# Six row products for four rows in the offset convolution, and its preparation one band earlier

## The chip, the cores and the metric

One core of a Trainium2 chip runs the whole kernel. The metric is the device time of one execution in microseconds. The engines are TensorE (PE; its weight loads are shown as PEld), VectorE (DVE), ScalarE (ACT), GpSimd (POOL) and SyncE (SP); POOL and SP also issue DMAs. Each engine takes its instructions in the order of the program.

## What is computed

Input x is 8 images of 128 channels by 64 x 64, all float32. Layer 0 normalises x by groups, computes 27 offset and mask channels with a 3 x 3 convolution, samples the image at the shifted places (a modulated deformable convolution), and adds the batch-normalised result to x. Layer 1 does a mixture of convolutions and isn't touched.

```python
om = conv3x3(gn(x), off_w) + off_b          # 27 channels a pixel
off, mask = om[:, :18], sigmoid(om[:, 18:])
val = bilinear samples of gn(x) at (y + ky - 1 + off_y, x + kx - 1 + off_x), times mask
y = sum over taps and channels of w * val + b
x = x + relu(batchnorm(y))
x = x + layer1(gn(x))
```

## The kernel before

**Bands.** `dense` walks over 64 bands, 8 (NB) for each image, each of 8 rows. `g` is the number of a band, `b, j` its image and its place in the image. A band has two parts. First come five sample groups: `weights` (L698) multiplies column and row weights on VectorE three groups ahead, `sample` runs the products on TensorE (L714, tile pq, three buffers) and ScalarE copies them away (L724). Then come the nine taps of the convolution of the band before it (`conv`, L763, tile py, one buffer). In band 0 the band before is the last of the previous image; it has two stretches of rows, and so eighteen matmul taps, which count as nine parts of two.

**Between the taps** the loop puts other work, by the number of the part (0 to 8). `pixels` (parts 0, 1, 5, 6) transposes picked pixels into pt (L672), and ScalarE copies them out (L677); pt and the tiles of the offset convolution share one buffer in ps_c. `spread` works on column weights, on ScalarE (L648, parts 1 and 5) and on VectorE (L650, parts 3 and 7). `pick` (L657) stands at part 4. `load_quarter` loads a quarter of the image two ahead, at part 4 of bands 2 to 5, on SP's queue.

**Loads of tables.** In the sample groups of each band POOL issues two column loads (`load_x`, L632) and eight row loads (`load_y`, L617).

**Tables of the next image but one.** `tables(b)` is a generator; after each tap the loop asks it for its next steps, three times (four in the first image's bands, and in band 0 three for each part of two taps). It yields BLOCK where it needs the shared buffer, and goes on from there only at the parts in BLOCKS. Its steps are: the group mean (pm, L309, and d, e, gm on VectorE), the group variance (pv, L319, and ve, L322), the power on POOL (L325), shift on VectorE (L328), the affine on the eight chunks of the image, in place, by turns on ScalarE (L332) and VectorE (L336), and then the offset convolution. `statistics(b)` (bn_stats, L294, and mv, L297) comes ahead of it.

**Offset convolution.** It takes two output rows at a time. Four combinations of input rows are made on VectorE (`combine`, L360, two halves of 128 x 1024 each), and each goes through 3 column taps x 4 quarters of the image, each quarter in 32 output columns of the array, on 8 rows of 64 (L379). The results are put together in om as even and odd rows (L402 to L415). om is turned by ScalarE (L422) and stored by SP's queue (L427, L432); later steps load it again (L465, L452) and make the tables (L503 to L564).

Of the kernel before, what the change touches and what calls it, by code (L numbers as in the profile page):

```python
# [8 lines left out]
F32 = mybir.dt.float32  # L9
I32 = mybir.dt.int32  # L10
AF = mybir.ActivationFunctionType
ALU = mybir.AluOpType
# [4 lines left out]
P = 128  # L17
H = W = 64
# [4 lines left out]
CH = 512  # L23
# [6 lines left out]
NE = 4  # L30
# [16 lines left out]
NB = NROW // 2  # L47
# [4 lines left out]
ROWPAD = REACH  # L52
# [4 lines left out]
BLOCK = "block"  # L57
# [7 lines left out]
def deform_moe_conv(  # L65
# [18 lines left out]
    nc = tc.nc  # L84
    B = x.shape[0]
# [92 lines left out]
    def dense():  # L178

        with ExitStack() as st:  # L180
# [16 lines left out]
            nc.gpsimd.memset(offw_sb[:, :, 27:32], 0.0)  # L197

            offu_sb = [a1.tile([P, 3, 32], F32, name=f"offu_sb{i}") for i in range(2)]
            offb_sb = a1.tile([P, 1], F32, name="offb_sb")  # L200
            nc.gpsimd.memset(offb_sb, 0.0)
            ident = a1.tile([P, P], F32, name="ident")
# [60 lines left out]
            def pause(n):  # L263
                for _ in range(n):
                    yield
# [34 lines left out]
            def tables(b):  # L300
# [22 lines left out]
                yield from pause(3)  # L323
                scale = small.tile([P, 1], F32, name="scale")
                nc.gpsimd.tensor_tensor(scale, ve, nhalf, ALU.pow)  # L325
                yield from pause(8)
                shift = small.tile([P, 1], F32, name="shift")
                nc.vector.scalar_tensor_tensor(shift, gm, -1.0, scale, ALU.mult, ALU.mult)  # L328
                yield
# [69 lines left out]
                for j in (1, 2):  # L399
                    yield from combine(j)  # L400
                yield from block(1)
                nc.scalar.activation(even, taken(1), AF.Identity, bias=offb_sb)  # L402
                yield from combine(0)
                yield from block(2)
                if b == 0:
                    yield from combine(3)
                m2 = taken(2)
                nc.vector.tensor_tensor(odd, even, m2, ALU.subtract)
                nc.vector.tensor_tensor(even, even, m2, ALU.add)
                if b:  # L410
                    yield from combine(3)
                yield from block(0)
                nc.vector.tensor_tensor(even, even, taken(0), ALU.add)
                yield from block(3)
                nc.vector.tensor_tensor(odd, odd, taken(3), ALU.subtract)  # L415
                yield
# [412 lines left out]
            load_x(2, nc.gpsimd)  # L829
            made, means_of = later, iter(())  # L830
            asked = False
            PIXELS, BLOCKS, SPREAD = (0, 1, 5, 6), (2, 3, 4, 7), (1, 3, 5, 7)

            def put_off():

# [10 lines left out]
            for g in range(len(bands) + 1):  # L846
                b, j = bands[g] if g < len(bands) else (B, 0)
                if j == NB - 2:
                    for _ in made:
                        pass  # L850
                    asked, made, means_of = True, iter(()), statistics(b + 2)
                turned = pixels(g + 1) if g + 1 < len(bands) else iter(())
                for q in range(NGR):
                    if g < len(bands):
                        if g or q + AHEAD < NGR:
                            weights(g * NGR + q + AHEAD)
                        sample(g * NGR + q)
                        if q == 2:
                            load_x(g + 3, nc.gpsimd)
                        if q in (2, 3):  # L860
                            for k in range(T * (q - 2), T * (q - 1)):
                                load_y(g + 2, k, nc.gpsimd)
                    if q == 1:
                        put_off()
                taps = conv(g - 1) if g else iter(())
                twice = 2 if g and bands[g - 1][1] == NB - 1 else 1
                for done, _ in enumerate(taps):
                    part, odd = divmod(done, twice)
                    if odd == 0 and part in PIXELS:
# [12 lines left out]
                    for _ in range(3 + (g < NB) if twice == 1 else 1 + done % 2):  # L882
                        tick()
                    if odd == 0 and part == 4:
                        if g + 2 < len(bands):
                            pick(g + 2)
                        if 2 <= j < 6:
                            load_quarter(b + 2, j - 2)
                for _ in turned:
                    pass  # L890
                if g == 0:
                    pick(2)
                    for slots in HALVES:
# [238 lines left out]


    def layer1():
        yscale = small.tile([P, 1], F32, name="yscale")
        rsqrt(yscale, ymv[:, 1:2], BN_EPS)
        nc.vector.tensor_tensor(yscale, yscale, gamma_sb, ALU.mult)
        yshift = small.tile([P, 1], F32, name="yshift")
        nc.vector.tensor_tensor(yshift, ymv[:, 0:1], yscale, ALU.mult)
        nc.vector.tensor_tensor(yshift, beta_sb, yshift, ALU.subtract)  # L1140
        with ExitStack() as st:
# [59 lines left out]
            def prepare(b, made):  # L1201
# [98 lines left out]
                tot = small.tile([P, 1], F32, name="tot")  # L1300
                nc.vector.tensor_reduce(tot, wd, AX.X, ALU.add)
                nc.vector.reciprocal(tot, tot)
                nc.vector.tensor_scalar(wd, wd, tot, None, ALU.mult)
                bmix = small.tile([P, 1], F32, name="bmix")

                def mix_biases():
                    mb = small.tile([P, NE], F32, name="mb")
# [194 lines left out]
```

## Time and profile before

| | |
|---|---|
| three timed runs, us | 1516.3, 1513.72, 1515.72; median 1515.72 |
| the profiled execution, us | 1504.96 (its span 1503.2) |
| mean granted TensorE clock | 0.969 |
| L379, offset convolution, after image 0 | 672 passes of 504 or 512 columns, 586 to 617 ns each, overlapping |
| L360, combinations on VectorE | 61 of 128x1024, 1229 ns, 73.3 us |
| L336 / L332, affine of a chunk, VectorE / ScalarE | 545 / 808 ns |
| L294, bn_stats of a chunk | 64, 678 ns |
| L325, power on POOL | 8, 647 ns |
| L677, copy of four transposed pixel tiles | 585 ns |
| L724, copy of a sample group | 923 or 1051 ns |
| column loads, row loads on POOL's queue | 576 KB each, 7.6 us to landing; 90 KB each, 8.1 us |

The profile describes one execution on the chip, and its times are from the span's start. A line of a timeline names the start, the length, the engine, the line of the kernel, the operation, the tiles written and read, and how many instructions were merged (x24); brackets give idle time of the engine ahead of it and what ended it. A float32 matmul shows as two passes. Matmuls are pipelined, so the length of one overlaps with the next; the distance between starts tells more.

### The profile page before, as it was taken

How to read it: one execution, taken by the hardware profiler on the slowest of the kernel's cores; microseconds unless marked ns; L12 is line 12 of the kernel's file. 1: busy time of each engine (PE TensorE's matmuls, PEld its weight loads, DVE VectorE, ACT ScalarE, POOL GpSimd, SP SyncE). 2: the span in 40 equal slices, each digit the busy share in tenths (PEclk: the TensorE clock that was granted, in tenths of full speed). 3: DMA queues.
4: the chain of work that ended last, by engine and by line, in shares of the span. 5: the costliest groups of instructions: out<-in, count | busy, mean ns of one | idle time of the engine just before them, and what ended most of it. 6: DMA issues, size and time to landing. Idle time of an engine off the chain costs nothing.

```text
span 1503.2 us, 21231 instructions
## 1 busy us (share of the span) xinstructions
PE 1363.5 (91%) x7714; PEld 761.6 (51%) x7714; DVE 959.3 (64%) x1906; ACT 818.3 (54%) x1095; POOL 449.9 (30%) x745
## 2 busy tenths in 40 slices
PE   4279799999999999999999899999994999999998
PEld 1245465556555555555556555566551444444443
DVE  5555475576557657656764775554528887888882
ACT  2365674776577468658656865866634232322320
POOL 6333242443334244333423333343303010110100
PEclk9589899999999999999999999999996999999999
DMA  4486775986697498669748866788708345665411
GB/s 143 115 181 126 175 163 105 213 190 137 128 202 179 95 196 214 137 130 207 187 99 183 194 147 135 168 183 200 171 26 248 93 124 149 168 168 154 110 45 58
DMA packets 130939, 227.27 MB, mean 151 GB/s; under 512 B 82003, under 2 KB 88303, under 8 KB 122137
## 3 DMA queue, kind: packets, MB, share of 16 engines
q0 software_dynamic: 54960, 137.08, 43.9%
q1 hardware_dynamic: 74848, 88.25, 19.9%
q8 instruction: 63, 1.03, 0.3%
q10 hardware_dynamic: 1017, 0.50, 0.1%
q14 instruction: 51, 0.42, 0.1%
HBM read 180.23 MB, written 45.35 MB: 150 GB/s over the span
## 4 chain that ended last, share of the span: by engine, by line
PE 53%; DMA 12%; ACT 9%; issue 9%; DVE 7%; SPq 2%; POOL 1%; ACTq 0%; DVEq 0%; POOLq 0%
PE py L763 20%; PE pc L1414 12%; PE pq L714 11%; PE pc L379 5%; PE pt L672 4%; DMA xwts<-tabx 4%; DMA pad<-in_x_dram 2%; ACT xwts L648 2%; ACT xt L677 2%; DMA combo<-colwise 2%; ACT work L537 1%; DMA x<-in_x_dram 1%; DMA yd<-y 1%; ACT samples L724 1%; DMA combo<-rowwise 1%
## 5 line engine op out<-in xcount | busy, mean ns | idle before, releaser
L763 PE MATMUL py<-samples,dw_sb 128*128 128x512 f32 (+3 forms) x1296 | 577.3, 562 | 7.1 <-ACT y L771 5.3
L617 POOL DMA_DIRECT2D ywts<-taby x504 | 305.5, 624 | 279.6 <-DMA xwts<-tabx 228.3
L714 PE MATMUL pq<-s,xt 64*128 64x144 f32 (+1 forms) x3840 | 283.8, 301 | 35.8 <-DVE s L698 24.7
L714 PEld LDWEIGHTS pq<-s,xt 64*128 64x128 f32 x3840 | 257.6, 190 | 84.7 <-ACT samples L724 24.2
L724 ACT COPY samples<-pq 128x864 f32<-128x864 f32 (+1 forms) x320 | 280.7, 974 | 33.6 <-PE pq L714 33.3
L763 PEld LDWEIGHTS py<-samples,dw_sb 128*128 128x128 f32 x1296 | 217.1, 190 | 160.3 <-issue 133.3
L677 ACT COPY xt<-pt 128x512 f32<-128x512 f32 (+1 forms) x256 | 142.4, 556 | 209.7 <-PE pt L672 209.2
L698 DVE TENSOR_TENSOR s<-xwts,ywts 128x72 f32<-128x72 f32 (+1 forms) x447 | 199.4, 499 | 84.6 <-PE pq L714 43.6
L650 DVE TENSOR_SCALAR xwts<-xwts 128x1152 f32<-128x1152 f32 (+2 forms) x130 | 97.3, 749 | 186.6 <-ACT xwts L648 186.2
L672 PEld LDWEIGHTS pt<-ident,picked 128*128 128x128 f32 x960 | 110.9, 141 | 171.7 <-ACT xt L677 105.0
L1414 PE MATMUL pc<-v,u 128*128 128x512 f32 x384 | 175.8, 605 | 6.3 <-DVE v L1321 6.3
L672 PE MATMUL pt<-ident,picked 128*128 128x128 f32 x960 | 152.8, 279 | 29.6 <-ACT xt L677 27.1
L632 POOL DMA_DIRECT2D xwts<-tabx x128 | 72.8, 573 | 353.5 <-DVE s L698 276.8
L1414 PE MATMUL pc<-v,wmix 128*128 128x512 f32 x384 | 174.0, 598 | 0.0
L648 ACT ACTIVATE xwts<-xwts,place 128x1152 f32<-128x1152 f32 (+2 forms) x130 | 160.9, 1242 | 11.5 <-DMA xwts<-tabx 11.5
L1392 ACT ACTIVATE t<-pc,bmix 128x512 f32<-128x512 f32 x32 | 22.0, 687 | 189.2 <-PE pc L1414 100.5
L1414 PEld LDWEIGHTS pc<-v,u 128*128 128x128 f32 x384 | 72.7, 192 | 93.5 <-issue 84.7
L1414 PEld LDWEIGHTS pc<-v,wmix 128*128 128x128 f32 x384 | 72.3, 190 | 91.4 <-issue 89.6
L360 DVE TENSOR_TENSOR combo<-pad 128x1024 f32<-128x1024 f32 x61 | 73.3, 1229 | 23.0 <-PE pc L379 14.4
L657 DVE COPY picked<-pad 128x960 f32<-128x960 f32 x128 | 81.9, 681 | 0.0
L771 ACT ACTIVATE y<-py,db_sb 128x512 f32<-128x512 f32 (+3 forms) x72 | 45.7, 635 | 65.6 <-PE py L763 31.1
L837 DVE BATCH_NORM_STATS2 ystats<-y 128x6 f32<-128x512 f32 (+3 forms) x72 | 44.5, 626 | 21.0 <-ACT y L771 21.0
(173 smaller groups left out, 955.3 us busy)
## 6 DMA issues: line engine op xcount, KB each, us to landing
xwts<-tabx POOLq DMA_DIRECT2D x128, 576.0 KB, 7.6
ywts<-taby POOLq DMA_DIRECT2D x504, 90.0 KB, 8.1
pad<-in_x_dram SPq DMA_DIRECT2D x36, 512.0 KB
out_dram<-yo SPq DMA_DIRECT2D x32, 512.0 KB
yd<-y SPq DMA_DIRECT2D x48, 256.0 KB
pad<-yd SPq DMA_DIRECT2D x16, 512.0 KB
x<-yd SPq DMA_DIRECT2D x16, 512.0 KB
x<-in_x_dram POOLq DMA_DIRECT2D x16, 512.0 KB, 9.2
```

What stands on the lines that cost most here:

```text
L379: nc.tensor.matmul(pcs[j][32 * q : 32 * q + 32].rearrange("p (h w) -> p h w", w=W)[:, :, lo:hi], lhsT=weight_of[j][:, kx], rhs=combo_of[j] ...
L617: engine.dma_start(out=y_wts[g % 2][at : at + NR * Q, r].rearrange("p a b c -> p (a b c)"), in_=bass.AP(tensor=y_table[b].tensor, offset=y ...
L648: nc.scalar.activation(part, part, AF.Abs, bias=column)
L650: nc.vector.tensor_scalar(part, part, -1.0, 0.0, ALU.add, ALU.min)
L657: nc.vector.tensor_copy(picked[g % 2][:, :, h], bass.AP(tensor=one.tensor, offset=one.offset, ap=[list(one.ap[0]), [T, NCOL], [W, Q], [1, Q]],
L672: nc.tensor.transpose(pt[:, c], picked[g % 2][:, c0 + c].rearrange("p h y x -> p (h y x)"), ident,)
L677: nc.scalar.copy(xts[g][:, c0 : c0 + n], pt[:, 0:n])
L698: engine.tensor_tensor(s[:, :, 3 * at : 3 * (at + k)].rearrange("p m (c x) -> p m c x", x=3), by_x[:, :, c : c + k], by_y[:, :, w : w + k] ...
L714: nc.tensor.matmul(by_m[:, h, :, at : at + k], lhsT=xts[g][rows, c], rhs=s[rows, :, at : at + k], start=True, stop=True,)
L724: nc.scalar.copy(bass.AP(tensor=one.tensor, offset=one.offset + first, ap=[list(one.ap[0]), [M * PLANE, 2], [PLANE, M], [WB + 1, 3], [1, w ...
L763: nc.tensor.matmul(py, lhsT=dw_sb[:, 3 * (2 - yy) + 2 - xx], rhs=samples[g % 2][:, m : m + 3 * n - 2 : 3, xx, 1 : W + 1], start=(i == 0), ...
L1414: nc.tensor.matmul(pc, lhsT=us[j][:, kx], rhs=vs[g][:, rows, kx : kx + W], start=(kx == 0), stop=(kx == 2),)
```

## The change

From the third image on (b of 2 and up) the offset convolution takes four output rows at a time: six combinations of six input rows, six products with six combinations of the three weight rows, and sums of the products. The combinations come in pairs, four VectorE operations each on 128 x 1024 (`combine_pair`); a pair of products (`pair`) shares a tile, 256 columns for each, and has 2 x 3 x 4 matmuls on 4 rows of 64. The six weight combinations (`quad_of`, `quad_weights`) are made once, after band 5 of image 0, in place, with one new tile. Images 0 and 1 keep the four products.

The steps ahead of the convolution are moved, for images 2 to 7. Counting the yields gives these places, with three steps a part (image 2, with four steps in bands 6 and 7, has its shift at part 1):

| step | before | after |
|---|---|---|
| bn_stats of chunks 0 to 5 | band 6, parts 0 to 5 | the same |
| bn_stats of chunks 6, 7, and mv | band 7, parts 0, 1 | band 6, part 6 |
| pm; d, e, gm | band 7, part 2 | band 6, part 7 |
| pv; ve | band 7, part 3 | band 6, part 8 |
| power on POOL | band 7, part 4 | band 7, part 0 |
| shift | band 7, part 7 | band 7, part 2 |
| affine chunks | band 7, parts 7, 8; band 0, part 0 | band 7, parts 2, 3, 4 |
| combinations | band 0, parts 1 to 3, 7, 8; band 1, parts 2, 3 | the first in band 7, part 8; seven in band 0, parts 0 to 4; four in band 1, parts 0 to 2 |
| products | block 1: band 0, part 7; blocks 2, 0, 3: band 1, parts 2, 4, 7 | pair 0: band 0, part 7; pairs 1, 2: band 1, parts 3, 7 |
| results into om | after each block | two after pair 0 (and one on ScalarE), two after pair 1 (and one on ScalarE), six after pair 2 |
| turning, stores and all that follows | from band 1, part 8 | the same |

Four small tiles of the layer-1 part get one buffer where they had two (not shown in the diff).

```diff
+            offv_sb = a1.tile([P, 3, 32], F32, name="offv_sb")
+            quad_of = (
+                offw_sb[:, 0:3], offu_sb[0], offu_sb[1], offw_sb[:, 3:6], offv_sb, offw_sb[:, 6:9]
+            )
...
-                yield from pause(8)
+                yield from pause(8 if b < 2 else 6)
                 shift = small.tile([P, 1], F32, name="shift")
...
+                PACE = 2, 2, 2
+                quad = omr.rearrange("p (t i w) -> p i t w", i=4, w=W)
+                halves = [(t[:, 0 : H // 4], t[:, H // 4 :]) for t in combos]
+                def row(k):
+                    return pad[:, ROWPAD - 1 + k :][:, 0 : H - 3 : 4]
+                def mix(out, a, times, c):
+                    if times in (1, -1):
+                        op = ALU.add if times == 1 else ALU.subtract
+                        nc.vector.tensor_tensor(out, c, a, op)
+                    else:
+                        nc.vector.scalar_tensor_tensor(out, a, float(times), c, ALU.mult, ALU.add)
+                def combine_pair(n):
+                    lo, hi = halves[n % 2]
+                    for args in (
+                        (
+                            (lo, row(2), -4, row(4)), (hi, row(1), -4, row(3)),
+                            (lo, hi, 1, lo), (hi, hi, -2, lo),
+                        ),
+                        (
+                            (lo, row(2), -1, row(4)), (hi, row(1), -1, row(3)),
+                            (lo, hi, 2, lo), (hi, hi, -4, lo),
+                        ),
+                        (
+                            (lo, row(2), -1.25, row(0)), (lo, row(4), 0.25, lo),
+                            (hi, row(3), -5, row(5)), (hi, row(1), 4, hi),
+                        ),
+                    )[n]:
+                        mix(*args)
+                        yield from pause(PACE[n])
+                def pair(n):
+                    yield BLOCK
+                    pc = ps_c.tile([P, CH], F32, name="pc", tag="pc")
+                    for i, j in enumerate(((1, 2), (3, 4), (0, 5))[n]):
+                        weight = quad_of[j]
+                        for kx in (1, 0, 2):
+                            lo, hi = max(0, 1 - kx), min(W, W + 1 - kx)
+                            for q in range(4):
+                                nc.tensor.matmul(
+                                    pc[32 * q : 32 * q + 32, CH // 2 * i : CH // 2 * (i + 1)]
+                                    .rearrange("p (h w) -> p h w", w=W)[:, :, lo:hi],
+                                    lhsT=weight[:, kx],
+                                    rhs=halves[n % 2][i][
+                                        :, 4 * q : 4 * q + 4, lo + kx - 1 : hi + kx - 1
+                                    ],
+                                    start=(kx == 1), stop=(kx == 2),
+                                    skip_group_check=True,
+                                )
+                    pcs[n] = pc.rearrange("p (i t w) -> p i t w", i=2, w=W)
+                    yield from pause(2)
...
+                if b < 2:
...
+                else:
+                    yield from pause(8)
+                    yield from combine_pair(0)
+                    yield from combine_pair(1)
+                    yield from pair(0)
+                    first, second = pcs[0][:, 0], pcs[0][:, 1]
+                    nc.scalar.activation(quad[:, 0], first, AF.Identity, bias=offb_sb)
+                    yield
+                    nc.vector.tensor_tensor(quad[:, 1], quad[:, 0], second, ALU.subtract)
+                    nc.vector.tensor_tensor(quad[:, 0], quad[:, 0], second, ALU.add)
+                    yield from pause(4)
+                    yield from combine_pair(2)
+                    yield from pair(1)
+                    first, second = pcs[1][:, 0], pcs[1][:, 1]
+                    nc.scalar.copy(quad[:, 3], first)
+                    yield from pause(2)
+                    nc.vector.tensor_tensor(quad[:, 2], quad[:, 3], second, ALU.add)
+                    nc.vector.tensor_tensor(quad[:, 3], quad[:, 3], second, ALU.subtract)
+                    yield from pair(2)
+                    first, second = pcs[2][:, 0], pcs[2][:, 1]
+                    for at, a, times, c in (
+                        (0, 2, 1, 0), (2, 2, 3, 0), (1, 3, 2, 1), (3, 3, 6, 1),
+                    ):
+                        mix(quad[:, at], quad[:, a], times, quad[:, c])
+                    nc.vector.tensor_tensor(quad[:, 0], quad[:, 0], first, ALU.add)
+                    nc.vector.tensor_tensor(quad[:, 3], quad[:, 3], second, ALU.add)
+                    yield
...
-            PIXELS, BLOCKS, SPREAD = (0, 1, 5, 6), (2, 3, 4, 7), (1, 3, 5, 7)
+            PIXELS, BLOCKS, SPREAD = (0, 1, 5, 6), (2, 3, 4, 7, 8), (1, 3, 5, 7)
+            def quad_weights():
+                v0, v1, v2, v3, v4, v5 = quad_of
+                nc.vector.tensor_tensor(v2, v0, v5, ALU.add)
+                nc.vector.tensor_tensor(v1, v2, v3, ALU.add)
+                nc.vector.tensor_tensor(v2, v2, v3, ALU.subtract)
+                nc.vector.scalar_tensor_tensor(v4, v5, 4.0, v0, ALU.mult, ALU.add)
+                nc.vector.scalar_tensor_tensor(v3, v3, 2.0, v4, ALU.mult, ALU.add)
+                nc.vector.scalar_tensor_tensor(v4, v4, 2.0, v3, ALU.mult, ALU.subtract)
+                for v, n in ((v1, -6.0), (v2, -6.0), (v3, 24.0), (v4, 24.0)):
+                    nc.scalar.activation(v, v, AF.Copy, scale=1.0 / n)
...
-                    if odd == 0 and (j == NB - 2 and part < 6 or j == NB - 1 and part < 2):
-                        next(means_of, None)
-                    if odd == 0 and j == NB - 1 and part == 2 and b + 2 < B:
+                    if odd == 0 and j == NB - 2 and part < 7:
+                        for _ in range(2 if part == 6 else 1):
+                            next(means_of, None)
+                    if odd == 0 and j == NB - 2 and part == 7 and b + 2 < B:
                         made = tables(b + 2)
                         next(made)
...
+                if g == 5:
+                    quad_weights()
```

More of the change, by code (lines that the diff above doesn't have):

```diff
@@ L397, in block @@
                     yield from pause(2)
[L399 to L416, printed above, removed]
+                PACE = 2, 2, 2
[3 more added lines that the diff above has]
+                    return pad[:, ROWPAD - 1 + k :][:, 0 : H - 3 : 4]
@@ new lines, in tables @@
+                if b < 2:
+                    for j in (1, 2):
+                        yield from combine(j)
+                    yield from block(1)
+                    nc.scalar.activation(even, taken(1), AF.Identity, bias=offb_sb)
+                    yield from combine(0)
+                    yield from block(2)
+                    if b == 0:
+                        yield from combine(3)
+                    m2 = taken(2)
+                    nc.vector.tensor_tensor(odd, even, m2, ALU.subtract)
+                    nc.vector.tensor_tensor(even, even, m2, ALU.add)
+                    if b:
+                        yield from combine(3)
+                    yield from block(0)
+                    nc.vector.tensor_tensor(even, even, taken(0), ALU.add)
+                    yield from block(3)
+                    nc.vector.tensor_tensor(odd, odd, taken(3), ALU.subtract)
+                    yield
[25 more added lines that the diff above has]
+                    nc.vector.tensor_tensor(quad[:, 3], quad[:, 3], second, ALU.add)
+                    yield
@@ L1134, in layer1 @@
     def layer1():
-        yscale = small.tile([P, 1], F32, name="yscale")
+        yscale = small.tile([P, 1], F32, name="yscale", bufs=1)
         rsqrt(yscale, ymv[:, 1:2], BN_EPS)
         nc.vector.tensor_tensor(yscale, yscale, gamma_sb, ALU.mult)
-        yshift = small.tile([P, 1], F32, name="yshift")
+        yshift = small.tile([P, 1], F32, name="yshift", bufs=1)
         nc.vector.tensor_tensor(yshift, ymv[:, 0:1], yscale, ALU.mult)
@@ L1299, in prepare @@
                 )
-                tot = small.tile([P, 1], F32, name="tot")
+                tot = small.tile([P, 1], F32, name="tot", bufs=1)
                 nc.vector.tensor_reduce(tot, wd, AX.X, ALU.add)
@@ L1306, in mix_biases @@
                 def mix_biases():
-                    mb = small.tile([P, NE], F32, name="mb")
+                    mb = small.tile([P, NE], F32, name="mb", bufs=1)
                     nc.vector.tensor_tensor(mb, eb_sb, wd, ALU.mult)
```

## The prediction

> **What bounds the kernel now.** I read the page's header and chain first, then the image periods, then the timelines of single engines around one image boundary.
>
> ```profile
> span 1503.2 us, 21231 instructions
> PE 1363.5 (91%) x7714; PEld 761.6 (51%) x7714; DVE 959.3 (64%) x1906; ACT 818.3 (54%) x1095; POOL 449.9 (30%) x745
> PE py L763 20%; PE pc L1414 12%; PE pq L714 11%; PE pc L379 5%; PE pt L672 4%; DMA xwts<-tabx 4%; DMA pad<-in_x_dram 2%; ACT xwts L648 2%; ACT xt L677 2%; DMA combo<-colwise 2%; ACT work L537 1%; DMA x<-in_x_dram 1%; DMA yd<-y 1%; ACT samples L724 1%; DMA combo<-rowwise 1%
> ...
> 484.35:613.88 129.53, 125.53 (x863) 74.58 (x863) 83.50 (x168) 88.33 (x118) 49.48 (x82) 1.00 0.75 167
> ```
>
> The last line is one image of the dense part (columns: length, then busy us of PE, PEld, DVE, ACT, POOL, then granted clock, DMA share, GB/s). TensorE works 125.53 of 129.53 us, so whatever takes work from it, or makes it wait, moves the end one for one. The offset convolution is L379, 5% of the chain. What can go wrong shows in the boundary between bands 7 and 0 (the first three lines are POOL's, then DVE, ACT, PE):
>
> ```profile
> 734.94 0.92 POOL L617 DMA_DIRECT2D ywts<-taby  x1 [3.36 <-DMA xwts<-tabx]
> 737.90 0.56 POOL L617 DMA_DIRECT2D ywts<-taby  x1 [2.04 <-DMA xwts<-tabx]
> 738.48 1.19 POOL L325 TENSOR_TENSOR scale<-ve,nhalf 128x1 f32<-128x1 f32 x1
> ...
> 734.45 0.16 DVE L322 TENSOR_SCALAR ve<-pv 128x1 f32<-128x1 f32 x1
> 739.71 0.16 DVE L328 SCALAR_TENSOR_TENSOR shift<-gm,scale 128x1 f32<-128x1 f32 x1 [0.43 <-POOL scale L325]
> ...
> 739.90 2.23 ACT L332 ACTIVATE pad<-pad,shift,scale 128x512 f32<-128x512 f32 x3 [1.04 <-DVE shift L328]
> ...
> 743.67 1.56 PE L714 MATMUL pq<-s,xt 64*128 64x144 f32 x20 [1.45 <-ACT samples L724]
> ```
>
> The variance was ready at 734.6, but the power that turns it into the scale ran at 738.48, the moment POOL had got rid of the band's eighth row-weight load, which itself waited for the two column-weight loads to land. Band 7 had begun at 724.58, so the power came 13.9 us into a band of 14.
>
> **The products.** Before, an image has four products, each 24 TensorE passes of 504 or 512 columns. One of them, and its weight loads:
>
> ```profile
> 638.09 2.83 PE L379 MATMUL pc<-combo,offu_sb 128*32 128x512 f32 x24
> ...
> 638.09 0.23 PEld L379 LDWEIGHTS pc<-combo,offu_sb 128*32 128x32 f32 x8 [0.67 <-ACT xt L677]
> 638.54 0.20 PEld L379 LDWEIGHTS pc<-combo,offu_sb 128*32 128x32 f32 x4 [0.22 <-issue]
> ```
>
> The next convolution pass starts at 640.85, so a product occupies 2.76 us: six rounds of four passes side by side, 0.43 us between the groups of loads (638.54, 638.97, ...), and the last of them a little longer. Four products are 10.9 us. After, three pairs make 12 rounds each of 252 or 256 columns. Half of 0.43 is 0.215; four loads occupy 0.20, and at the start eight went in 0.23, so they fit under it. Lower bound: 12 x 0.215 = 2.6 us a pair. Upper bound by a row with smaller passes: 60 passes of L714 take 4.13 us where their 9216 columns, two rows side by side at 512 columns in 0.43, would be 3.87, so 4 ns more a pass; 48 x 4 ns is 0.2, 2.8 a pair. By the far row, if the 109 ns of one load did not overlap with the others, 48 x 0.109 = 5.2 a pair. I take 2.75: that row is also a small-pass stream with a load per pass, and the loads are seen to overlap. An image saves 10.9 - 8.25 = 2.6, six images **-15.7 us** (-18.6 to -15; +28 by the far bound).
>
> The Trainium skill ("TensorE: Matmul & The Clock Gate", Part 3, What overlaps and what doesn't) says that a weight load overlaps running matmuls only where the row group differs, which speaks against this change, as all groups here use 128 rows. By it each round would be 0.20 + 0.215 us, a pair 5.0, an image 15: a loss of 4. But the eight loads in 0.23 us, two rounds' worth, ran while the first passes streamed, and the round period is 0.43 and not 0.63, so the trace speaks against the rule.
>
> **Statistics and group mean in band 6.** Eight bn_stats (0.59 pitch) now end in band 6, and pm waits for them at part 7. In the band begun at 710.62 the sixth was over at 723.6; two more and the mv (0.37) make 725.1, and PE is at part 7 at 723.6. It waits about 1.2 to 1.5, and in band 7 it no longer does (2.12, 0.67, 0.41, 1.48 us in four images, nothing in two). The last quarter of x must be there a few us sooner: it was issued at 709.88 and is needed at about 723, 13 us later, and 512 KB from the same tensor take 9.2 to 9.6 on POOL's queue. It is covered by some 4 us; if it landed as late as the chain's 16 us piece, PE would wait 3 more in that image.
>
> **Affine in band 7.** This is where I expect the loss. The power is still issued in band 7 (part 0), behind that band's two column and eight row loads, so its time does not move. But shift is now at part 2, where VectorE comes about 7 us into the band. VectorE stops there until the power is done; behind it stand four affine chunks, half a spread (L650), the pick and the other half. ScalarE stops at part 2 too: four affine chunks, and behind them the pixel copy of part 5. TensorE needs that copy, since ps_c has one buffer: its transposes of part 6 wait, normally 11.8 us into the band (678.58 in the band begun at 666.77).
>
> Worked for any image, P being the start of the power: power 0.57, shift and handing over 0.22, four ScalarE chunks at 0.715 pitch 2.85, pixel copy 0.59, so the transposes start at P + 4.3; to the next band's samples another 2.2 (680.77 - 678.58): P + 6.5. The P of the six are 214.68, 344.61, 477.28, 608.37, 738.48 (1.19 long, so 0.6 more) and 873.64: band 0 would start at 221.2, 351.1, 483.8, 614.9, 745.6, 880.1. Before, taking the start of the second sample group, after its wait, less the 2.60 of the first, it started in effect at 218.93, 348.55, 481.75, 611.28, 741.07, 876.79. The differences are 2.3, 2.6, 2.0, 3.6, 4.5, 3.3: 18.3 us. The later samples of band 7 also hold back its column loads (they wait for L698 on VectorE), by the 1.2 us in two images and by about 0.5 in the four where POOL was late anyway: 4.4. Together **+22.7 us**; this contains the waits of before that go away, and band 6's wait where it is swallowed. Bounds: 15, if the loads land as early as in the best band (power 11.2 after its start), to 30 with a 1.2 us power everywhere and later loads.
>
> **Combinations and results.** VectorE has twelve operations of 128x1024 for eight, 1.15 us apart (two L360 in 2.35). The first stands in band 7; seven stand in band 0, behind weights that end 5.0 into a band, with one spread (0.68) and the pick (1.2): 5.0 + 7 x 1.15 + 1.9 = 15.0, and TensorE is at the first pair at 15.0 (626.26 - 610.34, less the 0.93 of a wait that goes). A near tie: it waits 0 to 0.4 for the handing over and what VectorE carries over from band 7, **+2.4** at the upper of these. The four for the second pair stand in band 1: 5.2 + 4 x 1.15 = 9.8, and PE gets to part 3 at 8.4 (638.09 is part 2, 7.6 after 630.46). **+1.5** an image with the handing over, **+9.0**. Where the fused form costs what L1342 does (1.415 for 1152, so 1.26 for 1024, at 1.18 pitch), 0.1 to 0.3 more. The 256-element results (0.42 each, between the 0.69 of 512 and the 0.23 of 72) are hidden: the four of the last step run while TensorE makes the third pair, two follow it and hold the turning copy, and with it the sample copies, by 0.25: **+1.5** in all. Without that cover they would cost 1.7 an image. The SP queue's stores and loads of the offsets follow the same positions and move with them. The weights' six small VectorE and four ScalarE operations come once, at the end of a band: under 2 us of other engines, nothing on the path. A buffer less in the small pool costs nothing that layer 1's rows show.
>
> **Sum.** -15.7 + 22.7 + 2.4 + 9.0 + 1.5 = +19.9 us on the profiled execution, 1504.96 (span 1503.2): 1525. The three timed runs have a median of 1515.72, 10.8 above it; carried over, **1535**. With the bounds this case reaches from +5 (-18.6 + 15 + 9) to +30 (-15 + 30 + 2.4 + 9 + 1.5, and 1.8 for dearer fused operations): 1521 to 1546.
>
> **Rivals.** (1) **The stall is covered** and it gets faster. If the power ends by about 8 us into band 7, transposes of part 6 do not wait, and then all that band 7 lost before goes: effective starts less 13.95 us of band, 1.5, 1.45, 3.7, 2.3, 2.5, 3.1, 14.6 together; band 6's wait takes 6 x 1.2 = 7.2 back. -15.7 - 14.6 + 7.2 + 2.4 + 9 + 1.5 = -10: 1506. For it: POOL's first six loads are out early in all bands. Against: in six images the power never began before 11.2. Chance 0.14. (2) **Loads of weights set the pace** of the half-length passes: +28 for -15.7, 1579. Against it stand the overlapping loads; 0.05. (3) **VectorE is the bound in bands 0 and 1**: if strided rows and two inputs cost 1.4 us an operation, the first pair waits 0.4 + 7 x 0.25 and the second 1.5 + 4 x 0.25: 16.5 more, 1552. The L360 rows already read strided rows at 1.15, which is against it; 0.11. (4) **Saving and waits cancel**: half of the band 7 stall and no wait at the pairs, within 3 us: 0.08. What remains, 0.62, is the forecast.
>
> **How the numbers follow.** A measurement here tells about 0.2%, 3 us, from no change. Slower has the forecast, (2) and (3): 0.78; same 0.08; faster 0.14. The range 1509 to 1553 takes in the forecast's own range, (3) and (4), and leaves out (1) and (2).
>
> **What would show it.** In the trace of after: pair passes of 2.6 to 2.8 us in groups of 48; a wait of VectorE on L325 of 4 us or more at the shift in band 7, a wait of PE's transposes on the pixel copy of 3 to 6 us there; a wait of pm in band 6 of 1.2; a wait of PE on the last combination in band 1 of about 1.5; image periods 3 us longer. If the shift doesn't wait, the forecast falls; if the pairs take 5 us, the first term does.

## The result, and the profile after

After the change the median of five runs is 1534.92 us (1528.17 to 1536.9), before 1515.72 (1503.69 to 1516.77). The ratio is 1.0134 with an interval of 1.0089 to 1.0178: the kernel is slower, by less than 2%. A ratio is the mean of a kernel's runs over the mean of the runs of the kernel before beside it, without those more than 1.5% above the fastest of their kernel, so it isn't the quotient of the two medians. The profiled execution took 1528.17 us with a span of 1526.4, against 1504.96 and 1503.2: 23.2 us more of span. The mean granted clock of TensorE is 0.956, against 0.969.

The page's header, its busy times and the first lines of its chain of waits:

```profile
span 1526.4 us, 21856 instructions
PE 1362.0 (89%) x8002; PEld 779.9 (51%) x8002; DVE 995.9 (65%) x1972; ACT 820.7 (54%) x1105; POOL 441.1 (29%) x745
PE 50%; DMA 13%; issue 8%; DVE 7%; ACT 5%; POOL 1%; SPq 0%; DVEq 0%; POOLq 0%; ACTq 0%
PE py L855 18%; PE pc L1521 13%; PE pq L806 11%; DMA xwts<-tabx 4%; PE pt L764 4%; PE pc L450 3%; DMA ywts<-taby 3%; DMA combo<-rowwise 2%; ACT xt L769 1%; ACT xwts L740 1%; DVE stats L299 1%; DMA x<-in_x_dram 1%; DVE s L790 1%; ACT pad L337 1%; DMA combo<-colwise 1%
```

TensorE's busy time is 1.5 us less than before in a span that is 23.2 longer. The new products (L450) have 3% of the chain where the old ones (L379) had 5%. So most of the time was lost in waiting. (Not all: the same 8002 passes take 1349.1 us where the six products stand without the moved steps, 12.9 us less than here; the granted clock comes into that, as is shown below.) The place is found by cutting both traces at the first sample pass of every band and comparing lengths. After minus before, us, rows are the images that TensorE works on:

| image | band 0 | band 1 | bands 2 to 4 | band 5 | band 6 | band 7 |
|---|---|---|---|---|---|---|
| 0 | 0.2 | 0.9 | -0.3 | 0.4 | 1.8 | 5.3 |
| 1 | 0.8 | -3.5 | 1.4 | -1.5 | 1.9 | 4.6 |
| 2 | -0.8 | -3.0 | 0.0 | -1.1 | 1.8 | 4.2 |
| 3 | -1.2 | -3.0 | 0.0 | 6.5 | 1.8 | 5.0 |
| 4 | -0.7 | -3.0 | 0.0 | 0.4 | 4.6 | 5.7 |
| 5 | -1.1 | -3.0 | 0.0 | -4.5 | 2.9 | 4.1 |
| 6 | -1.2 | -3.0 | 0.0 | 0.0 | 0.0 | 0.0 |

Bands 6 and 7 of the six images in which another is prepared lose 14.8 and 28.8 us, bands 0 and 1 of images 1 to 6 give back 4.2 and 18.5. Band 5 goes both ways: VectorE waits there for loads that land now early and now late, in the kernel before too.

**Band 7.** The timeline of the band begun at 748.13, one that was shown of the kernel before (the lines are POOL's, then DVE's, ACT's and PE's):

```profile
759.76 0.56 POOL L709 DMA_DIRECT2D ywts<-taby  x1 [2.51 <-DMA xwts<-tabx]
760.33 0.56 POOL L330 TENSOR_TENSOR scale<-ve,nhalf 128x1 f32<-128x1 f32 x1
...
760.93 0.16 DVE L333 SCALAR_TENSOR_TENSOR shift<-gm,scale 128x1 f32<-128x1 f32 x1 [7.07 <-POOL scale L330]
...
761.12 2.93 ACT L337 ACTIVATE pad<-pad,shift,scale 128x512 f32<-128x512 f32 x4 [3.41 <-DVE shift L333]
763.96 0.56 ACT L769 COPY xt<-pt 128x512 f32<-128x512 f32 x1
...
764.58 0.90 PE L764 MATMUL pt<-ident,picked 128*128 128x128 f32 x3 [3.81 <-ACT xt L769]
765.27 3.62 PE L855 MATMUL py<-samples,dw_sb 128*128 128x512 f32 x4
768.82 1.49 PE L806 MATMUL pq<-s,xt 64*128 64x216 f32 x8
```

Read it downwards as a relay. POOL gets rid of the eighth row load at 760.3, when the column loads have landed; only then does the power run. VectorE has stood at the shift for 7.07 us, ScalarE for 3.41; ScalarE's pixel copy comes behind four affine chunks, and TensorE has waited 3.81 for it. The last two lines show what comes after the wait: four passes that take 1.92 us elsewhere take 3.62. The busy time by stretches (the column with 0.91 and 0.50 is the granted clock) says why:

```profile
748.13:764.58 16.45, 12.64 (x88) 8.18 (x87) 8.10 (x20) 10.74 (x15) 6.31 (x11) 0.91 0.66 137
765.27:768.84 3.57, 3.57 (x7) 1.03 (x6) 2.42 (x3) 0.77 (x2) 0.00 (x0) 0.50 0.01 2
```

Behind the wait TensorE is granted half its clock. The same holds in all six bands: waits of 3.59, 3.71, 5.10, 4.13, 3.81 and 3.01 us, each with 3.4 or 6.8 us at 0.5 that begin within it or up to 0.9 us behind it, and the samples of band 0 start 3.4 to 4.3 us after the transposes instead of 2.2.

**Band 6.** PE's wait for the statistics in the same image:

```profile
745.85 0.35 PE L314 MATMUL pm<-mv,gsel 128*128 128x1 f32 x2 [3.13 <-DVE mv L302]
```

The six waits are 1.24, 1.32, 1.24, 1.24, 3.13 and 2.10 us, 10.3 together. In the last two, VectorE's sample weights, which stand ahead of the statistics, had waited 3.03 and 2.01 us for row weights and room, and the statistics came later by as much.

**The products.** The three pairs of the next image, on TensorE, and VectorE beside the second of them:

```profile
784.14 2.77 PE L450 MATMUL pc<-combo,offu_sb 128*32 128x256 f32 x48
786.84 1.58 PE L855 MATMUL py<-samples,dw_sb 128*128 128x256 f32 x6
...
796.75 1.49 PE L450 MATMUL pc<-combo,offw_sb 128*32 128x256 f32 x24
798.06 1.47 PE L450 MATMUL pc<-combo,offv_sb 128*32 128x256 f32 x24
799.45 1.80 PE L855 MATMUL py<-samples,dw_sb 128*128 128x448 f32 x4
...
803.89 2.77 PE L450 MATMUL pc<-combo,offw_sb 128*32 128x256 f32 x48 [0.21 <-ACT xt L769]
806.59 1.03 PE L855 MATMUL py<-samples,dw_sb 128*128 128x448 f32 x2
...
796.05 1.22 DVE L417 SCALAR_TENSOR_TENSOR combo<-pad 128x1024 f32<-128x1024 f32 x1
797.30 1.23 DVE L417 SCALAR_TENSOR_TENSOR combo<-pad,combo 128x1024 f32<-128x1024 f32 x1
```

From the start of a pair to the next pass are 2.70 us, three times. The second pair starts at 796.75 with no wait, while VectorE is still at the combinations (until 798.5) that were forecast to hold it back. No pair of the eighteen waits more than 0.21 us. In image 1 two of the three pairs stand in band 0.

### The profile page after: what moved, and what is told of

It is laid out like the page before. It is cut to its first block, busy times and chain, and to the rows that moved or that the text cites. A ratio compares the mean times of both kernels' runs of the same rounds, so it can differ in the third digit from the quotient of the medians.

```text
span 1526.4 us, 21856 instructions
## 1 busy us (share of the span) xinstructions
PE 1362.0 (89%) x8002; PEld 779.9 (51%) x8002; DVE 995.9 (65%) x1972; ACT 820.7 (54%) x1105; POOL 441.1 (29%) x745
## 4 chain that ended last, share of the span: by engine, by line
PE 50%; DMA 13%; issue 8%; DVE 7%; ACT 5%; POOL 1%; SPq 0%; DVEq 0%; POOLq 0%; ACTq 0%
PE py L855 18%; PE pc L1521 13%; PE pq L806 11%; DMA xwts<-tabx 4%; PE pt L764 4%; PE pc L450 3%; DMA ywts<-taby 3%; DMA combo<-rowwise 2%; ACT xt L769 1%; ACT xwts L740 1%; DVE stats L299 1%; DMA x<-in_x_dram 1%; DVE s L790 1%; ACT pad L337 1%; DMA combo<-colwise 1%
## 5 line engine op out<-in xcount | busy, mean ns | idle before, releaser
L855 PE MATMUL py<-samples,dw_sb 128*128 128x512 f32 (+3 forms) x1296 | 586.0, 571 | 7.1 <-ACT y L863 5.3
L709 POOL DMA_DIRECT2D ywts<-taby x504 | 297.2, 607 | 281.7 <-DMA xwts<-tabx 238.8
L806 PE MATMUL pq<-s,xt 64*128 64x144 f32 (+1 forms) x3840 | 286.2, 303 | 30.7 <-DVE s L790 28.2
L855 PEld LDWEIGHTS py<-samples,dw_sb 128*128 128x128 f32 x1296 | 221.5, 192 | 156.5 <-issue 129.4
L666 DVE TENSOR_TENSOR work<-work,combo 64x576 f32<-64x576 f32 x40 | 29.6, 748 | 40.8 <-ACT work L633 40.7
```

The source lines that it names most:

```text
L709: engine.dma_start(out=y_wts[g % 2][at : at + NR * Q, r].rearrange("p a b c -> p (a b c)"), in_=bass.AP(tensor=y_table[b].tensor, offset=y ...
L806: nc.tensor.matmul(by_m[:, h, :, at : at + k], lhsT=xts[g][rows, c], rhs=s[rows, :, at : at + k], start=True, stop=True,)
L855: nc.tensor.matmul(py, lhsT=dw_sb[:, 3 * (2 - yy) + 2 - xx], rhs=samples[g % 2][:, m : m + 3 * n - 2 : 3, xx, 1 : W + 1], start=(i == 0), ...
```

## The experiments

Nine runs. "Band lengths" are those of the table above; the same-chip ratios are against the kernel before.

**The products alone.** The six products stay; statistics, mean, power, shift and affine go back to their places of before.

```diff
-                yield from pause(8 if b < 2 else 6)
+                yield from pause(8)
-                PACE = 2, 2, 2
+                PACE = 2, 1, 2
...
                 else:
-                    yield from pause(8)
                     yield from combine_pair(0)
...
-            PIXELS, BLOCKS, SPREAD = (0, 1, 5, 6), (2, 3, 4, 7, 8), (1, 3, 5, 7)
+            PIXELS, BLOCKS, SPREAD = (0, 1, 5, 6), (2, 3, 4, 7), (1, 3, 5, 7)
...
-                    if odd == 0 and j == NB - 2 and part < 7:
+                    if odd == 0 and (j == NB - 2 and part < 6 or j == NB - 1 and part < 2):
+                        next(means_of, None)
+                    if odd == 0 and j == NB - 1 and part == 2 and b + 2 < B:
```

> The six products with the old places: statistics of chunks 6 and 7 and the group mean in band 7, shift at part 7, affine up to band 0. If the loss is all in the moved preparation, only the shorter products are left: 18.5 us less than before on the path (bands 0 and 1 of the changed kernel were shorter by that), so about 1497 where before has 1515.7, and no wait of VectorE on the power beyond 1 us. If VectorE's twelve combinations, now all in band 0 and 1 behind the affine, cost TensorE waits as I had forecast for the pairs (1.9 us an image), about 1509.

Measured: 1501.42 us against 1508.16, ratio 0.9925 (0.9882 to 0.9968); span 1489.1. Band 1 is 3.0 us shorter in images 2 to 6 and band 7 within 0.8 of before. So the six products by themselves are a gain, but not the whole of the 18.5 us: the span is 14.1 us shorter, and the ratio lies between the two expectations. The pairs don't wait here either. But in image 1 the gain is lost again, since the transposes that follow the first pair wait for its results, which VectorE takes out of the shared buffer only behind two more combinations and the pick:

```profile
234.88 1.09 PE L763 MATMUL pt<-ident,picked 128*128 128x128 f32 x4 [3.00 <-DVE om L490]
```

A second run of this kernel, beside the last experiment, has the same wait of 3.00 us in its trace; the traces of before and of the change don't have it.

> The six products with the steps ahead of them at their old places, again, beside the kernel above on the same chip: ratio about 0.9925, as before.

0.993 (0.9898 to 0.9963), span 1489.3.

**The places alone.** Four products as before for all images, with the steps ahead of them at their new places. The weight combinations have been overwritten by then, so the offsets that it computes are others; the work is the same.

```diff
-                if b < 2:
+                if b < 8:
+                    if b > 1:
+                        yield from pause(13)
```

> The four products of before with the new places of statistics, mean, power, shift and affine. If the moved preparation alone makes the loss, bands 6 and 7 lengthen as in the changed kernel, by 39.5 us over six images with band 0's part taken off: about 1555. If the pair's first combination in band 7 and the heavier VectorE share in it, clearly less: 1535 or below.

Measured: 1551.63 us, ratio 1.0286 (1.023 to 1.0342); span 1551.0. Band 7 is 30.7 us longer over six images, band 6 19.7, band 1 of images 2 to 6 unchanged. So the whole loss belongs to the places. (The two parts' spans, -14.1 and +47.8, add up to some 10 us more than the change's 23.2; 4.9 of it is band 6, where pm waited 5.55 us in one image behind late weights, and some 4 are bands 0 and 1 of image 1, where the products alone have the wait just shown.)

**The power ahead of band 7's loads.** One step moves, from part 0 of band 7 to part 8 of band 6; the shift stays.

```diff
-                yield from pause(3)
+                yield from pause(3 if b < 2 else 0)
                 scale = small.tile([P, 1], F32, name="scale")
                 nc.gpsimd.tensor_tensor(scale, ve, nhalf, ALU.pow)
-                yield from pause(8 if b < 2 else 6)
+                yield from pause(8 if b < 2 else 9)
```

> The changed kernel with the power issued in band 6 right behind ve, so ahead of band 7's ten loads on POOL; shift stays at part 2. If POOL's queue holds the power back, VectorE's waits on it (42.6 us in the profile) fall under 5 and band 7 gets back to about 14 us: 25 to 29 us less than the changed kernel, about 1508; the 15 us more in band 6, where PE waits for mv, stay. If instead the affine's own work on ScalarE ahead of the pixel copy is what TensorE waits for, band 7 stays 3 us too long: 1520 or more.

Measured: 1504.92 us, ratio 0.996 (0.9921 to 0.9998); span 1502.9. The timeline of this kernel at the same boundary (POOL, DVE, PE; the band began at 734.8):

```profile
734.56 0.56 POOL L709 DMA_DIRECT2D ywts<-taby  x1 [1.92 <-DMA xwts<-tabx]
735.29 0.76 POOL L330 TENSOR_TENSOR scale<-ve,nhalf 128x1 f32<-128x1 f32 x1 [0.17 <-DVE ve L327]
737.09 1.19 POOL L724 DMA_DIRECT2D xwts<-tabx  x2 [1.04 <-DVE s L790]
...
739.78 0.16 DVE L333 SCALAR_TENSOR_TENSOR shift<-gm,scale 128x1 f32<-128x1 f32 x1
...
747.06 0.55 PE L764 MATMUL pt<-ident,picked 128*128 128x128 f32 x3 [0.29 <-ACT xt L769]
747.45 1.92 PE L855 MATMUL py<-samples,dw_sb 128*128 128x512 f32 x4
```

The power now starts 0.5 us into the band, in front of the band's loads, and VectorE finds the scale ready. The transposes wait 0.29 and the four passes behind them take 1.92. Band 7 is 14.5 us in four images, 15.3 and 16.0 in the others: the 28.8 us are gone with this one step. Band 6 keeps its loss, 1.8 to 2.2 us in four images and 8.3 and 6.7 in two, where VectorE's weights had waited 6.34 and 4.20 us for row loads.

**Is the slow clock a cost of its own?** Four matmuls whose results nobody uses fill the wait: to the kernel after the change in one run, to the kernel with the power ahead, which has a wait of 0.3 us there, in the other.

```diff
+                    if j == NB - 1 and part == 6 and b + 2 < B:
+                        spare = ps_q.tile([P, 2, CH], F32, name="pq")
+                        for _ in range(4):
+                            nc.tensor.matmul(
+                                spare[:, 0], lhsT=ident,
+                                rhs=dw_sb.rearrange("p k o -> p (k o)")[:, 0:CH],
+                                start=True, stop=True,
+                            )
```

> The changed kernel with four matmuls more of 128x512 (3.5 us of TensorE) in band 7 just ahead of the transposes of part 6, where TensorE waits 3.8 us; their result is not used. If TensorE's lower clock after such a wait costs time of its own, the work that fills the wait makes the kernel faster, by 1.7 us or more an image, 10 us in all: about 1525. If the clock has no part, it stays within 2 us of the changed kernel's 1535 or gets slower.

> The four idle matmuls of e4 put into e3, where TensorE has no wait in band 7 to fill. The clock theory says that e4's band 7 got 1.5 us shorter only because the work filled a wait and kept the clock up: here each band 7 must get longer by the matmuls' 3.5 us, 21 us in all over e3 (1.010 of before). If the matmuls are cheaper than that for another reason, band 7 lengthens by less than 2 us and the clock isn't shown by e4.

First the changed kernel with the added matmuls (L976), then the control:

```profile
764.62 2.31 PE L976 MATMUL pq<-dw_sb,ident 128*128 128x512 f32 x5
768.72 0.55 PE L764 MATMUL pt<-ident,picked 128*128 128x128 f32 x3 [1.80 <-ACT xt L769]
769.11 1.92 PE L855 MATMUL py<-samples,dw_sb 128*128 128x512 f32 x4
```

```profile
753.73 3.59 PE L976 MATMUL pq<-dw_sb,ident 128*128 128x512 f32 x8
757.16 0.49 PE L764 MATMUL pt<-ident,picked 128*128 128x128 f32 x3
757.49 1.92 PE L855 MATMUL py<-samples,dw_sb 128*128 128x512 f32 x4
```

With the wait filled, the passes behind it take 1.92 us and no stretch at half clock follows any of the six bands 7. Those bands are 18.0, 17.9, 19.0, 18.7, 19.4 and 19.3 us long, against 19.8, 19.1, 20.9, 20.3, 20.7 and 20.2: 8.7 us less, with more work in them. From the transposes to the samples of band 0 it is 2.23 us in all six, where the change has 3.4 to 4.3: 10.6 us less over six images, of which 2.0 are lost because the transposes themselves start later. In the control the same matmuls make band 7 longer: 17.4 us in five images (14.5 in four of them without, 15.3 in one), 19.2 for 16.0 in the last, 2.8 us each where 3.5 was expected. So the half clock is paid on top of the wait, 1.2 to 2.0 us each time. The totals don't show it clearly: 1528.15 us, ratio 1.0112 (1.0056 to 1.0169), where 1525 was expected, because bands 5 and 6 of images 2 to 5 had longer load waits in its trace; the control has 1518.53, 1.0069 (1.0026 to 1.0111). The bands are the evidence. The change itself was run again beside the control:

> The changed kernel once more, beside the others on the same chip: bands 6 and 7 of images 0 to 5 longer than before's by 2 to 5 us and 4 to 6 us, half-clock stretches behind band 7's wait, a ratio to before of 1.009 to 1.018.

1531.84 us, 1.0177 (1.0117 to 1.0237), which overlaps with the first ratio. In its trace the bands 6 are longer than before by 1.8 us in five images and by 2.6 in one, the bands 7 by 3.4 to 6.1. In image 0 the transposes wait 3.67 us, as long as elsewhere, and no stretch at half clock follows:

```profile
223.03 0.55 PE L764 MATMUL pt<-ident,picked 128*128 128x128 f32 x3 [3.67 <-ACT xt L769]
223.42 1.92 PE L855 MATMUL py<-samples,dw_sb 128*128 128x512 f32 x4
```

There the samples of band 0 come 2.23 us after the transposes, in the other five images 3.7 to 4.25. So the same kernel shows the wait with and without the slow clock, and the difference is of the size that the added matmuls gave. It shows as well that a wait of this length doesn't always bring the clock down.

**Band 6: earlier statistics.** To the power ahead, six of the eight bn_stats are moved off the end of band 6: chunks 0 to 3 to band 5, 4 and 5 to the start of band 6.

```diff
+                if j == NB - 3:
+                    means_of = statistics(b + 2)
-                    if odd == 0 and j == NB - 2 and part < 7:
-                        for _ in range(2 if part == 6 else 1):
-                            next(means_of, None)
+                    if odd == 0 and (j == NB - 3 and part > 4 or j == NB - 2 and part in (0, 1, 4, 5)):
+                        next(means_of, None)
```

> The kernel of e3 (power ahead of band 7's loads) with the eight statistics spread out: chunks 0 to 3 in band 5 (parts 5 to 8), 4 and 5 at parts 0 and 1 of band 6, 6 and 7 at parts 4 and 5. If band 6's loss in the changed kernel (14.8 us, and 22.7 in e3's profile) comes from mv standing at the end of VectorE's work in that band, behind sample weights that wait for row loads, PE's wait for mv falls under 0.5 us and band 6 gets back to 14: 15 to 20 us less than e3, a ratio to before of about 0.985, and a shorter time than e1's. If it comes from the mean's matmuls standing in band 6 at all, band 6 stays 1.5 us or more too long and the ratio stays near e3's 0.996.

1497.37 us, ratio 0.9927 (0.9892 to 0.9963). The wait at pm is down to 0.1 us in five images and 0.76 in the sixth, but four of the six bands 6 now have TensorE waiting 0.99 us for sample weights near their start, and that of image 0 1.69, since the statistics at the end of band 5 make VectorE late with those. Of the four bands 6 that were 1.8 to 2.2 us over before without this edit, three are still at 1.9 and one at 0.7; the two that were 8.3 and 6.7 over it are at 1.9 and 2.5. By the ratios the gain over the kernel without this edit is 0.0033, where 0.011 was expected, and the two intervals overlap. The regular wait was moved more than removed. In this trace VectorE has no long wait for row loads in any band 6, so that the two large losses are gone is not shown to be the edit's doing.

**Band 6: two chunks only, in band 4**, where VectorE is not behind; the other six in band 6, parts 0 to 5.

```diff
+                if j == NB - 4:
+                    means_of = statistics(b + 2)
-                    if odd == 0 and j == NB - 2 and part < 7:
-                        for _ in range(2 if part == 6 else 1):
-                            next(means_of, None)
+                    if odd == 0 and (j == NB - 4 and part in (2, 3) or j == NB - 2 and part < 6):
+                        next(means_of, None)
```

> The kernel of the experiment with the power ahead of band 7's loads, with bn_stats of chunks 0 and 1 in band 4 (parts 2, 3), where VectorE has room, and chunks 2 to 7 in band 6, parts 0 to 5, so that mv is done some 4 us ahead of part 7. If band 6's remaining loss (1.8 to 2.2 us an image, 6 to 8 in two) is VectorE's lateness with mv alone, band 6 returns to its length of before in all six images, band 7 stays at 14.5, and the ratio is 0.985 to 0.988 (band 1 and bands 7 to 0 shorter by about 20 us, nothing given back). If the loss comes from late row loads that hold up VectorE's weights, the 1.8 us go in four images and the 6 to 8 us stay in those where the loads are late: 0.988 to 0.993. If statistics in band 4 delay that band's weights as they did in band 5, band 4 or 5 grows by 1 us an image instead and the ratio is about 0.993.

1496.76 us, ratio 0.9895 (0.9846 to 0.9945). Three of the six bands 6 have no wait of TensorE at all and are 0.7 us longer than before, what pm, pv and their neighbours now take there. One waits 0.66 for sample weights near its start. Two have a wait at pm, 1.26 and 5.07 us, and in both VectorE's weights had waited for row loads, 3.26 and 6.16 us. Where the larger comes from is DVE's first line here (lines of DVE, then PE):

```profile
847.29 1.81 DVE L790 TENSOR_TENSOR s<-xwts,ywts 128x432 f32<-128x432 f32 x4 [6.16 <-DMA ywts<-taby]
...
853.85 0.67 DVE L299 BATCH_NORM_STATS2 stats<-pad 128x6 f32<-128x512 f32 x1
854.55 0.37 DVE L302 BATCH_NORM_AGGREGATE mv<-stats 128x2 f32<-128x48 f32 x1
...
855.07 0.56 PE L314 MATMUL pm<-mv,gsel 128*128 128x1 f32 x2 [5.07 <-DVE mv L302]
```

A row load that lands 6.16 us late on VectorE reaches TensorE through mv as 5.07. Before the change pm stood four parts later, and its waits were 0.41 to 2.12. So the second reading of the expectation holds: the regular 1.2 us at pm were VectorE's, and the large ones are late row loads; when those are late was not found out. This is the fastest version, with a gain that its interval keeps away from none; from the products alone on the same chip (0.993) it can't be told apart.

## Why the prediction was right, and by what

The forecast of 1535 us with a sum of +19.9 was met by 1534.92, and +23.2 in the profiled execution. The direction and the main place of the loss were right. That the number was met so closely is luck: two groups of terms were off, by 15.7 and 16.7 us, in opposite ways:

| term | forecast | measured | where it is measured |
|---|---|---|---|
| products | -15.7 | -18.5, with the waits of the pairs (the passes alone: -16.2) | band 1, images 1 to 6 |
| waits of the pairs, results | +2.4 +9.0 +1.5 | none seen | the same |
| affine, group mean and their effect on band 0 | +22.7 | +39.4 | bands 6 and 7, band 0 of images 1 to 6 |
| the rest | 0 | +2.3 | bands 2 to 5, and 0 and 1 of image 0 |

**Products: right.** 2.75 us a pair was taken, 2.70 is measured in 17 of 18 pairs (2.88 in the other); the bounds of 2.6 and 2.8 held for them. Four products took 10.8 us (2.69 three times and 2.76), so an image saves 2.7 us of passes. The rule that spoke against the change, that a weight load overlaps running matmuls only where the row group differs (the Trainium skill, "TensorE: Matmul & The Clock Gate", Part 3, What overlaps and what doesn't), would have made it 5.0 by the prediction's estimate. This trace doesn't agree with it: all groups have the same 128 rows, and yet 48 loads of 0.11 us are hidden under 48 passes of 252 or 256 columns.

**Waits of the pairs: wrong.** The failed step is "the four for the second pair stand in band 1": that put the third set of combinations ahead of the second pair. The code has `rhs=halves[n % 2]`: pair 0 reads the first four combinations, pair 1 the second four, made in band 0, and only pair 2 those of band 1. The set made in band 1 overwrites what pair 0 read, which TensorE is done with. So each pair has a set to spare, and pair 0 had 4 operations less ahead of it than the forecast's 15.0 us. The 11.4 us of these two waits were a misreading of the code, not of the chip. The 1.5 for the results didn't show in band 1 either.

**Band 7: right in sum and in mechanism, with two sizes off inside.** Forecast: 18.3, and 4.4 for late column loads, and the 6.3 us of band 0's waits that the effective starts had taken off, 29.0 in all; measured 28.8. The transposes come 4.25 us after the start of the power in all six images, as worked out (P + 4.3). But the power itself started 11.3 to 12.8 us into the band, 71.5 over six bands, where 77.0 and the 4.4 were reckoned: the columns were not held back, and part of band 6's wait was most likely used by the loads under way. And the step "to the next band's samples another 2.2" failed: it is 3.4 to 4.3 us, 10.8 more over six images, because TensorE comes out of the wait at half clock. That cost was not priced at all; the power's earlier start made up for it, and this is luck too.

**Band 6: the term that was mis-sized.** The failed step is that the 22.7 "contains [...] band 6's wait where it is swallowed". It is not swallowed: the band 7 that follows begins later and its loads with it. Band 6 costs 14.8 us: 10.3 of waits at pm, larger than the 1.2 to 1.5 forecast in the two images with late weights, and about 0.7 an image for pm and pv, which are now in this band. Band 0 gave back 4.2 and not 6.3.

**The signs that were named**: the pairs' length, VectorE's wait at the shift (6.7 to 7.3, 4 or more was named), the transposes' wait (3.0 to 5.1; 3 to 6) and the pm wait (1.24 in three images) came as written; the wait on the last combination in band 1 did not. Image periods 3 us longer came only in the mean (3.8): those of images 1 to 5 changed by -1.6 to +9.1 us, most of the spread being band 5.

**Rivals.** That the stall is covered is refuted by the 7 us waits; the run with the power ahead shows what it would have been worth. That weight loads set the pace is refuted by 2.70, that VectorE is the bound in bands 0 and 1 by the pairs that start without a wait; what VectorE's share in them did cost in a trace is the 3.00 us of image 1 in the products alone.

The prediction's 0.2%, 3 us, for telling a change from none was too small: single executions of the kernel before spread over 13 us and more, and the intervals of the ratios reach 0.3 to 0.6% to either side.

What stays open: what late loads of bands 5 and 6 depend on, which moves single executions by 5 to 10 us, why one of the waits in band 7 left the clock up, and whether the last kernel is faster than the products alone.

## What to carry to other kernels

A step that is moved has to be placed against every in-order queue that it passes through: this one was moved nearer to its user on VectorE, while its input still came from an engine that had eight loads to get rid of first. For every product, read from the code which buffer it reads, not in which order the buffers are made. And a wait of TensorE of 3 us or more is to be priced with the passes behind it at half clock: here eleven of twelve such waits in band 7, in two traces of the same kernel, cost 1.2 to 2.0 us more than the wait.

## What the runs showed of the hardware

The granted clock fell to 0.5 for 3.4 or 6.8 us at every one of the six band 7 waits of 3.01 to 5.10 us in the first trace of the change, and behind the pm waits of 3.13 and 2.10, but at none of the four of 1.24 to 1.32. In the second trace it fell at five of the six and not at one of 3.67; in the trace of before it fell at a wait of 4.51 and not at those of 2.12, 2.34 and 2.95. So between 2.1 and 3.7 us these traces show both. Four passes took 3.62 us for 1.92. The Trainium skill ("TensorE: Matmul & The Clock Gate", Why this matters for your kernels) has the rule that matmul bursts should have no idle gaps of more than about 3 us between them. The six waits of band 7 in the first trace agree with it; the 2.10 us at pm, behind which the clock fell too, lie below its number, and the 3.67 us, behind which it didn't, above it.
